# Transposing only the even column tiles of a deformable convolution, and copying the odd ones inside SBUF

## The chip, the cores and the metric

The kernel runs on one core of a Trainium2 chip. A core has a matrix engine (TensorE, PE in the profile), a vector engine (VectorE, DVE), a scalar engine (ScalarE, ACT), a general engine (GpSimd, POOL) and a queue engine (SyncE, SP), and 16 DMA engines that move data between the chip's memory (HBM) and the core's on-chip memory SBUF, or inside SBUF. SBUF has 128 partitions. TensorE writes to a small second memory, PSUM, from which ScalarE or VectorE copies results to SBUF. DMAs are issued from the queues of SP, ScalarE and GpSimd. The metric is the time of one execution on the device in microseconds (us); lower is better.

## The reference

The input `x` is 8 images of 128 channels and 64x64 pixels, in float32. There are two layers, each added to its input. Layer 0 is a group norm, a modulated deformable 3x3 convolution, a batch norm and a ReLU. Layer 1 is a group norm and a routed mixture of 3x3 convolutions. The change touches layer 0 alone. Cut to what matters:

```python
om  = conv3x3(x, off_w) + off_b                 # 27 maps: 18 offsets, 9 masks
py  = off[:, :, 0] + row + ky ; px = off[:, :, 1] + column + kx
val = corner(y0, x0, (1-ly)*(1-lx)) + corner(y0, x0+1, (1-ly)*lx) \
    + corner(y0+1, x0, ly*(1-lx))   + corner(y0+1, x0+1, ly*lx)
val = val * sigmoid(mask)                       # 9 samples for each pixel and channel
y   = einsum('bckhw,ock->bohw', val, w) + b     # then batch norm, ReLU
```

For each pixel and each of nine taps the sample is a bilinear mix of the four pixels around a shifted position, and all 128 channels are mixed alike. The weight of a pixel at distance `d` in one direction is max(0, 1 - |d|).

## The kernel before

**Tiles.** An image is cut into 8 bands of 8 rows (`NB`), each of two halves of `T` = 4 rows. Across, there are `NCOL` = 15 column tiles that begin every 4 columns and are `Q` = 8 columns wide, so that neighbours share 4 columns. A patch of one half and one column tile is 8x8 = 64 pixels, so the two halves of a column tile fill 128 partitions: partition = 64 h + 8 y + x. All samples whose offset stays below 2 pixels (`REACH`) lie inside their patch. A program that finds larger offsets takes another path, which doesn't run here.

**A band.** Five steps lead from the image to the output of a band.

1. `pick` (L748, VectorE, two copies of 128x960) takes the 15 patches of the normalised image in `pads` into one of two `picked` buffers, channels on partitions.
2. `pixels` (L761) turns them with TensorE, one 128x128 transpose for each column tile, in groups of 4, 4, 4 and 3. A group goes into one PSUM bank, `pt` (tag "pc", one buffer, which other work shares), and ScalarE copies it to `xt` (L773). `xt` has pixels on partitions and channels along the row; there are two such buffers.
3. The weights in x come from a table in HBM (`x_table`). `load_x` (L722) reads one row of 9216 bytes for each half and spreads it over 64 partitions, as two GpSimd DMAs, into one of three `x_wts` buffers. `spread` (L738) makes weights of it: ScalarE takes |distance - column of this partition| (the bias `column`), VectorE subtracts 1 and clips at 0. It works on the two halves of the row (`HALVES`) one after the other. The weights in y are loaded by `load_y` (L706), eight GpSimd DMAs a band into one of two `y_wts` buffers.
4. `weights` (L779, VectorE) multiplies both into `s`, for three column tiles at a time, and `sample` (L800) multiplies `xt` by `s` on TensorE: 30 products a band, 60 matmul instructions. ScalarE copies them into `samples` (L820).
5. `conv` (L847) is the convolution proper: nine taps of 128x128 weights (18 matmul instructions for a span of rows), one ScalarE copy to `y`, one SP DMA of `y` to HBM (L869).

**Order.** Everything in this stage is in an order written out by hand. The loop over 64 bands (and one more turn) at L954 samples band `g`, and then runs the convolution of band `g - 1`, with other work placed between its nine steps: the transposes of band `g + 1` at steps 0, 1, 5 and 6 (`PIXELS`), `load_x` of `g + 3` at step 2, the Abs and clip of the halves of band `g + 2` at steps 1, 3, 5 and 7 (`SPREAD`), and `pick` of `g + 2` at step 4. The y loads of `g + 2` are issued during the sampling. The first and last bands of an image have their convolution in two spans. The generator `tables` makes the offset maps and tables of the image after the next, a small piece at every `tick`; it uses all engines, and SP for its DMAs.

**Start.** Before the loop the tables of image 0 are made in one go (L871 to L920), with the first transposes (L694), the first y loads from the SP and ScalarE queues (L697), and the weights of the first band.

Of the kernel before, what the change touches and what calls it, by code (L numbers as in the profile page):

```python
# [47 lines left out]
GT = 3  # L48
NGR = NCOL // GT
M = 3 * T  # L50
WB = W + 2
# [13 lines left out]
def deform_moe_conv(  # L65
# [113 lines left out]
    def dense():  # L179

        with ExitStack() as st:
# [10 lines left out]

            picked = [a1.tile([P, NCOL, 2, Q, Q], F32, name=f"picked{i}") for i in range(2)]
            for t in pads:
# [31 lines left out]

            place_i = a1.tile([P, 2], I32, name="place_i")
            place = a1.tile([P, 2], F32, name="place")
            beside = a1.tile([P, 1], F32, name="beside")
            nc.gpsimd.iota(place_i, pattern=[[REACH, 2]], base=Q - REACH, channel_multiplier=1)  # L230
            for i, n in ((0, T), (1, Q)):
                nc.vector.tensor_single_scalar(
                    place_i[:, i : i + 1], place_i[:, i : i + 1], n - 1, op=ALU.bitwise_and
                )
            nc.vector.tensor_copy(place, place_i)
# [6 lines left out]
            nc.vector.tensor_tensor(place[:, 0:1], place[:, 0:1], beside, ALU.add)  # L242
            nc.vector.tensor_scalar(place[:, 1:2], place[:, 1:2], -1.0, None, ALU.mult)
            in_tile, column = place[W:P, 0:1], place[:, 1:2]

# [60 lines left out]
            def tables(b):  # L306
# [224 lines left out]
                if b == 0:  # L531
                    for g in range(2):
                        pick(g)
                nc.vector.tensor_reduce(
                    most[:, b : b + 1], omr, AX.X, ALU.max, apply_absolute_value=True
# [155 lines left out]
                for i in (3, 0, 4, 1, 2):  # L691
                    masked(i)
                    store_y(i, 1, soon)
                for _ in pixels(0):  # L694
                    pass
                for k in range(2 * T):
                    load_y(0, k, nc.scalar if k in (1, 4, 7) else nc.sync)  # L697
                for _ in statistics(1):
                    pass
                for slots in ((NCOL * T, XROW // XSTEP), (0, 12), (12, 36), (36, NCOL * T)):  # L700
                    spread(0, slots)
                store_x(2, 6, nc.gpsimd)
# [19 lines left out]
            def load_x(g, engine):  # L722

                if g >= len(bands):
                    return
                b, j = bands[g]
                for h in range(2):
                    engine.dma_start(  # L728
                        out=x_wts[g % 3][HALF * h : HALF * h + HALF],
                        in_=bass.AP(  # L730
                            tensor=x_table[b].tensor,
                            offset=x_table[b].offset + (2 * j + h) * XROW,
                            ap=[[0, HALF], [1, XROW]],
                        ),
                    )


            def spread(g, slots=(0, XROW // XSTEP), steps_=(0, 1)):  # L738

                if g >= len(bands):  # L740
                    return
                part = x_wts[g % 3][:, slots[0] * XSTEP : slots[1] * XSTEP]
                if 0 in steps_:
                    nc.scalar.activation(part, part, AF.Abs, bias=column)  # L744
                if 1 in steps_:
                    nc.vector.tensor_scalar(part, part, -1.0, 0.0, ALU.add, ALU.min)  # L746

            def pick(g):  # L748

                b, j = bands[g]  # L750
                for h in range(2):
                    one = pads[b % 2][:, 2 * T * j + T * h : 2 * T * j + T * h + 1, 0:1]
                    nc.vector.tensor_copy(  # L753
                        picked[g % 2][:, :, h],
                        bass.AP(
                            tensor=one.tensor, offset=one.offset,
                            ap=[list(one.ap[0]), [T, NCOL], [W, Q], [1, Q]],
                        ),
                    )

            def pixels(g):  # L761

                xts[g] = a2.tile([P, NCOL, P], F32, name="xt")
                for c0 in range(0, NCOL, 4):
                    n = min(4, NCOL - c0)
                    pt = ps_c.tile([P, 4, P], F32, name="pt", tag="pc")
                    for c in range(n):
                        nc.tensor.transpose(  # L768
                            pt[:, c],
                            picked[g % 2][:, c0 + c].rearrange("p h y x -> p (h y x)"),  # L770
                            ident,
                        )
                    nc.scalar.copy(xts[g][:, c0 : c0 + n], pt[:, 0:n])  # L773
                    yield

            def width(q):
# [23 lines left out]
            def sample(n):  # L800
# [5 lines left out]
                for c in range(GT * q, GT * q + GT):  # L806
                    k = 3 * (T + 2 * (c in (0, NCOL - 1)))
                    for h in range(2):
                        rows = slice(HALF * h, HALF * h + HALF)
                        nc.tensor.matmul(  # L810
                            by_m[:, h, :, at : at + k],
                            lhsT=xts[g][rows, c],
                            rhs=s[rows, :, at : at + k],
                            start=True, stop=True,
                        )
                    at += k
# [102 lines left out]
            for n in range(AHEAD):  # L919
                weights(n, nc.vector if n < AHEAD - 1 else nc.gpsimd)  # L920
            HALVES = (0, 32), (32, 64)
            load_x(1, nc.gpsimd)
# [4 lines left out]
            asked = False  # L927
            PIXELS, BLOCKS, SPREAD = (0, 1, 5, 6), (2, 3, 4, 7, 8), (1, 3, 5, 7)

# [24 lines left out]
            for g in range(len(bands) + 1):  # L954
                b, j = bands[g] if g < len(bands) else (B, 0)
                if j == NB - 2:
                    for _ in made:
                        pass
                    asked, made, means_of = True, iter(()), statistics(b + 2)
                turned = pixels(g + 1) if g + 1 < len(bands) else iter(())  # L960
                if j == NB - 1:
# [13 lines left out]
                for done, _ in enumerate(taps):  # L975
# [5 lines left out]
                    if odd == 0 and part in SPREAD:  # L981
                        half, step = divmod(SPREAD.index(part), 2)
                        spread(g + 2, HALVES[half], (step,))
                    if odd == 0 and j == NB - 2 and part in (0, 1, 2, 4):
# [10 lines left out]
                    if odd == 0 and part == 4:  # L995
                        if g + 2 < len(bands):
                            pick(g + 2)
                        if 3 <= j < 6:
# [3 lines left out]
                for _ in turned:  # L1002
                    pass
                if g == 0:
                    load_x(3, nc.gpsimd)
                    pick(2)
                    for slots in HALVES:
                        spread(1, slots)
                    for n in range(AHEAD):
                        weights(NGR + n)  # L1010
                    for slots in HALVES:
                        spread(2, slots)
                if g == 5:
# [604 lines left out]
```

## Time and profile before

| | |
|---|---|
| Median of 3 runs | 1461.16 us (1460.37 to 1461.41) |
| The profiled execution, its own time | 1462.95 us |
| Its span, first to last instruction | 1461.2 us |
| Mean granted TensorE clock | 0.972 |
| TensorE matmuls, busy | 1339.4 us, 92% of the span |
| VectorE, ScalarE, GpSimd, busy | 996.1, 826.9 and 439.7 us |
| Bytes moved | 227.32 MB, mean 156 GB/s |
| Transposes (L768) | 960 |
| Copies of `xt` (L773) | 256, 142.0 us busy |
| x loads (L728) | 128 of 576 KB, median 7.7 us from issue to landing |
| y loads (L713) | 512 in all queues, 90 KB each |

A line of instructions is read as: source line, engine, operation, tiles written and read, shape, and count; then busy time and mean duration in ns of one; then how long the engine sat idle just before, and what ended that idle time. Matmuls are pipelined, so the durations of neighbours overlap. Idle time of an engine that isn't the bottleneck costs nothing. The rows of digits give the busy share in 40 equal slices of the span, in tenths.

### The profile page before, as it was taken

The page shows a single profiled execution, that of the slowest core. Times are in us where ns is not written, and L with a number is a line of the kernel's source. Part 1 is how long each engine was busy: PE and PEld are TensorE (multiplying, and loading weights), DVE is VectorE, ACT ScalarE, POOL GpSimd, SP SyncE. Part 2 cuts the span into 40 slices and gives each one's busy share as a digit, 9 for nine tenths or more (in the row PEclk, how much of TensorE's full clock was granted, in tenths as well). Part 3 has the DMA queues.
Part 4 walks back from the last instruction along what each step waited for, and adds up shares of the span by engine and source line. Part 5 has one row for each costly group of instructions (what it writes and reads, how often), then busy time and mean ns, then how long its engine had stood idle before and what let it go on. Part 6 is the DMA issues. An engine that isn't in the chain of part 4 may idle for free.

```text
span 1461.2 us, 21972 instructions
## 1 busy us (share of the span) xinstructions
PE 1339.4 (92%) x8002; PEld 766.7 (52%) x8002; DVE 996.1 (68%) x1986; ACT 826.9 (57%) x1117; POOL 439.7 (30%) x745
## 2 busy tenths in 40 slices
PE   4169989999999999999999999999976999999998
PEld 1144556656556656656656566565642444444443
DVE  5546687678668757857866686654528887888872
ACT  2365875777687577668668757866633333232320
POOL 6243333433435234333534433343212101011000
PEclk9579999999999999999999999999997999999999
DMA  4494874884687497577758756677418544565411
GB/s 147 94 187 121 178 182 127 191 209 127 160 212 181 127 204 189 145 175 200 177 131 196 189 147 162 169 186 194 139 39 238 143 125 129 149 173 163 111 44 60
DMA packets 120144, 227.32 MB, mean 156 GB/s; under 512 B 73142, under 2 KB 76370, under 8 KB 111338
## 3 DMA queue, kind: packets, MB, share of 16 engines
q0 software_dynamic: 55024, 137.08, 40.7%
q1 hardware_dynamic: 64795, 88.25, 19.9%
q8 instruction: 65, 1.06, 0.3%
q14 instruction: 53, 0.43, 0.1%
q10 hardware_dynamic: 207, 0.50, 0.1%
HBM read 180.23 MB, written 45.35 MB: 154 GB/s over the span
## 4 chain that ended last, share of the span: by engine, by line
PE 55%; ACT 6%; DMA 5%; issue 5%; DVE 3%; POOL 2%; SPq 0%; DVEq 0%; POOLq 0%; ACTq 0%
PE pc L1530 20%; PE py L859 18%; PE pq L810 10%; PE pt L768 4%; PE pc L453 3%; POOL ywts L713 2%; DMA xwts<-tabx 2%; ACT xwts L744 1%; ACT xt L773 1%; DMA taby<-work 1%; DMA ywts<-taby 1%; ACT pad L340 1%; DMA x<-in_x_dram 1%; ACT om L515 1%; ACT samples L820 1%
## 5 line engine op out<-in xcount | busy, mean ns | idle before, releaser
L859 PE MATMUL py<-samples,dw_sb 128*128 128x512 f32 (+3 forms) x1296 | 573.1, 560 | 7.1 <-ACT y L867 5.3
L713 POOL DMA_DIRECT2D ywts<-taby x504 | 295.9, 608 | 563.5 <-DVE s L794 468.8
L820 ACT COPY samples<-pq 128x864 f32<-128x864 f32 (+1 forms) x320 | 281.3, 976 | 32.0 <-PE pq L810 32.0
L859 PEld LDWEIGHTS py<-samples,dw_sb 128*128 128x128 f32 x1296 | 217.5, 189 | 152.8 <-issue 122.5
L810 PE MATMUL pq<-s,xt 64*128 64x144 f32 (+1 forms) x3840 | 279.7, 299 | 19.0 <-DVE s L794 13.2
L810 PEld LDWEIGHTS pq<-s,xt 64*128 64x128 f32 x3840 | 253.9, 188 | 62.3 <-DVE xwts L746 22.5
L746 DVE TENSOR_SCALAR xwts<-xwts 128x1152 f32<-128x1152 f32 (+2 forms) x130 | 97.4, 749 | 196.8 <-ACT xwts L744 187.3
L794 DVE TENSOR_TENSOR s<-xwts,ywts 128x72 f32<-128x72 f32 (+1 forms) x447 | 199.3, 498 | 43.4 <-PE pq L810 40.1
L773 ACT COPY xt<-pt 128x512 f32<-128x512 f32 (+1 forms) x256 | 142.0, 555 | 143.9 <-PE pt L768 142.7
L768 PEld LDWEIGHTS pt<-ident,picked 128*128 128x128 f32 x960 | 111.2, 141 | 176.3 <-ACT xt L773 110.0
L768 PE MATMUL pt<-ident,picked 128*128 128x128 f32 x960 | 152.5, 279 | 33.7 <-ACT xt L773 31.1
L1530 PE MATMUL pc<-v,u 128*128 128x512 f32 x384 | 174.2, 600 | 6.3 <-DVE v L1437 6.3
L1530 PE MATMUL pc<-v,wmix 128*128 128x512 f32 x384 | 173.1, 596 | 0.0
L744 ACT ACTIVATE xwts<-xwts,place 128x1152 f32<-128x1152 f32 (+2 forms) x130 | 161.0, 1242 | 18.9 <-DMA xwts<-tabx 18.9
L1508 ACT ACTIVATE t<-pc,bmix 128x512 f32<-128x512 f32 x32 | 22.0, 687 | 187.5 <-PE pc L1530 98.9
L1530 PEld LDWEIGHTS pc<-v,u 128*128 128x128 f32 x384 | 71.8, 191 | 92.9 <-issue 83.1
L1530 PEld LDWEIGHTS pc<-v,wmix 128*128 128x128 f32 x384 | 72.0, 189 | 90.9 <-issue 88.9
L867 ACT ACTIVATE y<-py,db_sb 128x512 f32<-128x512 f32 (+3 forms) x72 | 45.8, 636 | 73.3 <-PE py L859 36.4
L728 POOL DMA_DIRECT2D xwts<-tabx x128 | 73.7, 592 | 31.5 <-DMA ywts<-taby 20.2
L753 DVE COPY picked<-pad 128x960 f32<-128x960 f32 x128 | 81.3, 676 | 0.0
L664 DVE TENSOR_TENSOR work<-work,combo 64x576 f32<-64x576 f32 x40 | 29.6, 746 | 44.8 <-ACT work L631 44.8
L945 DVE BATCH_NORM_STATS2 ystats<-y 128x6 f32<-128x512 f32 (+3 forms) x72 | 44.4, 625 | 20.1 <-ACT y L867 20.1
(199 smaller groups left out, 1043.1 us busy)
## 6 DMA issues: line engine op xcount, KB each, us to landing
xwts<-tabx POOLq DMA_DIRECT2D x128, 576.0 KB, 7.7
ywts<-taby POOLq DMA_DIRECT2D x504, 90.0 KB, 3.8
pad<-in_x_dram SPq DMA_DIRECT2D x36, 512.0 KB
out_dram<-yo SPq DMA_DIRECT2D x32, 512.0 KB
yd<-y SPq DMA_DIRECT2D x48, 256.0 KB
pad<-yd SPq DMA_DIRECT2D x16, 512.0 KB
x<-yd SPq DMA_DIRECT2D x16, 512.0 KB
x<-in_x_dram POOLq DMA_DIRECT2D x16, 512.0 KB, 9.1
```

Source lines behind the costliest of these rows:

```text
L713: engine.dma_start(out=y_wts[g % 2][at : at + NR * Q, r].rearrange("p a b c -> p (a b c)"), in_=bass.AP(tensor=y_table[b].tensor, offset=y ...
L728: engine.dma_start(out=x_wts[g % 3][HALF * h : HALF * h + HALF], in_=bass.AP(tensor=x_table[b].tensor, offset=x_table[b].offset + (2 * j + ...
L744: nc.scalar.activation(part, part, AF.Abs, bias=column)
L746: nc.vector.tensor_scalar(part, part, -1.0, 0.0, ALU.add, ALU.min)
L753: nc.vector.tensor_copy(picked[g % 2][:, :, h], bass.AP(tensor=one.tensor, offset=one.offset, ap=[list(one.ap[0]), [T, NCOL], [W, Q], [1, Q]],
L768: nc.tensor.transpose(pt[:, c], picked[g % 2][:, c0 + c].rearrange("p h y x -> p (h y x)"), ident,)
L773: nc.scalar.copy(xts[g][:, c0 : c0 + n], pt[:, 0:n])
L794: engine.tensor_tensor(s[:, :, 3 * at : 3 * (at + k)].rearrange("p m (c x) -> p m c x", x=3), by_x[:, :, c : c + k], by_y[:, :, w : w + k] ...
L810: nc.tensor.matmul(by_m[:, h, :, at : at + k], lhsT=xts[g][rows, c], rhs=s[rows, :, at : at + k], start=True, stop=True,)
L820: nc.scalar.copy(bass.AP(tensor=one.tensor, offset=one.offset + first, ap=[list(one.ap[0]), [M * PLANE, 2], [PLANE, M], [WB + 1, 3], [1, w ...
L859: nc.tensor.matmul(py, lhsT=dw_sb[:, 3 * (2 - yy) + 2 - xx], rhs=samples[g % 2][:, m : m + 3 * n - 2 : 3, xx, 1 : W + 1], start=(i == 0), ...
L1530: nc.tensor.matmul(pc, lhsT=us[j][:, kx], rhs=vs[g][:, rows, kx : kx + W], start=(kx == 0), stop=(kx == 2),)
```

## The change

Neighbouring column tiles share half of their columns: the 8 even tiles together hold every column once, and each odd tile consists of the last 4 columns of one even tile and the first 4 of the next. In the changed kernel `pick` and `pixels` handle the 8 even tiles only. A new function `share` makes the 7 odd tiles from them with eight DMAs, one for each column `x`: for this column it copies 16 partitions (2 halves and 8 rows), 7 tiles of 128 channels each (3584 bytes a partition), to the same partitions of the odd part of `xt`. As the partitions stay the same, an odd tile has its two groups of 4 columns exchanged, and `spread` uses a second bias for odd tiles. Its Abs is split into even and odd tiles rather than into two halves of the row, and the even part into two instructions.

In the loop the transposes are made two bands ahead, at steps 0 and 1 only; `share` is issued on SP's queue at step 3; both parts of the Abs stand at steps 1 and 3, the two clips at 5 and 7; `pick` is made three bands ahead. At the start, the transposes of the first two bands come right after their `pick`, the eight transfers of each are issued from ScalarE's queue, and the first y loads are dealt to SP, GpSimd, ScalarE and GpSimd in turn.

The source of an x load is written as eight groups of eight repeats of the row instead of 64 repeats. The bytes are the same.

```diff
+EVEN = (NCOL + 1) // 2
...
-            place_i = a1.tile([P, 2], I32, name="place_i")
...
+            for i, base, mask in ((0, T - REACH, T - 1), (1, 0, Q - 1), (2, T, Q - 1)):
+                one = place_i[:, i : i + 1]
+                nc.gpsimd.iota(one, pattern=[[0, 1]], base=base, channel_multiplier=1)
+                nc.vector.tensor_single_scalar(one, one, mask, op=ALU.bitwise_and)
...
                     for g in range(2):
                         pick(g)
+                        for _ in pixels(g):
+                            pass
+                    pick(2)
...
-                for _ in pixels(0):
-                    pass
+                for g in range(2):
+                    share(g, nc.scalar)
                 for k in range(2 * T):
-                    load_y(0, k, nc.scalar if k in (1, 4, 7) else nc.sync)
+                    load_y(0, k, (nc.sync, nc.gpsimd, nc.scalar, nc.gpsimd)[k % 4])
...
-                            ap=[[0, HALF], [1, XROW]],
+                            ap=[[0, Q], [0, Q], [1, XROW]],
...
+            def spread(g, tiles=(0, NCOL + 1), sides_=(0, 1), clip=True):
...
+                part = x_wts[g % 3].rearrange("p (c k) -> p c k", c=NCOL + 1)
+                for side in sides_:
+                    first = tiles[0] + (tiles[0] + side) % 2
+                    if first < min(tiles[1], NCOL):
+                        some = part[:, first : min(tiles[1], NCOL) : 2]
+                        nc.scalar.activation(some, some, AF.Abs, bias=columns[side])
+                    if side == 0 and tiles[1] > NCOL:
+                        some = part[:, NCOL]
+                        nc.scalar.activation(some, some, AF.Abs, bias=columns[side])
+                if clip:
+                    some = part[:, tiles[0] : tiles[1]]
+                    nc.vector.tensor_scalar(some, some, -1.0, 0.0, ALU.add, ALU.min)
...
-                            ap=[list(one.ap[0]), [T, NCOL], [W, Q], [1, Q]],
+                            ap=[list(one.ap[0]), [Q, EVEN], [W, Q], [1, Q]],
...
+                for c0 in range(0, EVEN, 4):
...
+            def share(g, engine):
+
+                if g >= len(bands):
+                    return
+                for x0 in range(T):
+                    for side in range(2):
+                        rows = slice(x0 + T * side, P, Q)
+                        engine.dma_start(
+                            out=xts[g][rows, EVEN:].rearrange("p c n -> p (c n)"),
+                            in_=xts[g][rows, 1 - side : EVEN - side].rearrange("p c n -> p (c n)"),
+                        )
...
-                            lhsT=xts[g][rows, c],
+                            lhsT=xts[g][rows, c // 2 + EVEN * (c % 2)],
...
-            PIXELS, BLOCKS, SPREAD = (0, 1, 5, 6), (2, 3, 4, 7, 8), (1, 3, 5, 7)
+            PIXELS, BLOCKS, SPREAD = (0, 1), (2, 3, 4, 7, 8), (1, 3, 5, 7)
...
-                turned = pixels(g + 1) if g + 1 < len(bands) else iter(())
+                turned = pixels(g + 2)
...
-                        half, step = divmod(SPREAD.index(part), 2)
-                        spread(g + 2, HALVES[half], (step,))
+                        step, half = divmod(SPREAD.index(part), 2)
+                        if step:
+                            spread(g + 2, HALVES[half], ())
+                        else:
+                            spread(g + 2, sides_=(half,), clip=False)
+                    if odd == 0 and part == 3:
+                        share(g + 2, nc.sync)
...
-                        if g + 2 < len(bands):
-                            pick(g + 2)
+                        pick(g + 3)
...
                 if g == 0:
+                    share(2, nc.sync)
                     load_x(3, nc.gpsimd)
-                    pick(2)
-                    for slots in HALVES:
-                        spread(1, slots)
+                    pick(3)
+                    spread(1)
```

## The prediction

> **What bounds the kernel now.** I read three views in this order: the slices and costliest groups of the page, busy time by stretch, and the timeline of one band. The page first.
>
> ```profile
> span 1461.2 us, 21972 instructions
> ...
> PE   4169989999999999999999999999976999999998
> ...
> L768 PE MATMUL pt<-ident,picked 128*128 128x128 f32 x960 | 152.5, 279 | 33.7 <-ACT xt L773 31.1 <-DVE picked L753 2.6
> ...
> L744 ACT ACTIVATE xwts<-xwts,place 128x1152 f32<-128x1152 f32 (+2 forms) x130 | 161.0, 1242 | 18.9 <-DMA xwts<-tabx 18.9
> ...
> L753 DVE COPY picked<-pad 128x960 f32<-128x960 f32 x128 | 81.3, 676 | 0.0
> ```
>
> TensorE (PE) is full from slice 4 to the end of the banded stage, near 1066 us; the transposes are 152.5 us of that. PE sat idle before them for 33.7 us only. The view by stretch (length, then busy time and count of PE, weight loads, DVE, ACT, POOL; clock; DMA share; GB/s) takes a heavy band of ScalarE, the two longest kinds, the start, and bands 4 on:
>
> ```profile
> 532.00:547.00 15.00, 14.53 (x96) 8.72 (x97) 9.84 (x24) 13.97 (x21) 5.62 (x10) 1.00 1.01 242
> ...
> 609.70:628.60 18.90, 18.90 (x192) 11.16 (x191) 15.42 (x31) 11.02 (x15) 5.94 (x10) 1.00 0.49 128
> ...
> 72.00:110.00 38.00, 25.95 (x174) 18.26 (x176) 18.50 (x36) 22.99 (x28) 18.92 (x32) 0.77 0.89 182
> ...
> 151.90:1050.00 898.10, 875.14 (x6411) 545.47 (x6410) 614.93 (x1252) 642.93 (x858) 340.16 (x584) 1.00 0.70 173
> ```
>
> PE is busy 875.14 of 898.10 us, so what PE no longer issues is time saved until another engine takes over. Next are ScalarE (0.72 on average, 13.97 of 15.00 in some bands) and the transfers (0.70). At the start, 72 to 110 us, the transfers lead (0.89). One light band on PE:
>
> ```profile
> 774.41 3.67 PE L859 MATMUL py<-samples,dw_sb 128*128 128x512 f32 x8
> 777.92 0.60 PE L768 MATMUL pt<-ident,picked 128*128 128x128 f32 x4
> 778.36 1.04 PE L859 MATMUL py<-samples,dw_sb 128*128 128x512 f32 x2
> 779.24 0.51 PE L768 MATMUL pt<-ident,picked 128*128 128x128 f32 x3
> 779.58 1.92 PE L859 MATMUL py<-samples,dw_sb 128*128 128x512 f32 x4
> ```
>
> From the start of a transpose group to the next convolution matmul: 778.36 - 777.92 = 0.44 us for four, 779.58 - 779.24 = 0.34 us for three. The durations overlap (0.60 for the first), so I price by starts.
>
> **What the Trainium skill says.** "SBUF — State Buffer", Door 1: 64 consecutive partitions reach 8 of 16 ports, measured 196 GB/s. The trace agrees: between 56.9 and 63.0 us, with the first pair of x loads and little else, the view by stretch has 206 GB/s. "DMA: Bandwidth & Descriptors", on why a DMA increments by 16: a transfer uses the largest number of engines up to 16 that divides both slowest dimensions. With 64 groups that is 16 engines a load, with eight groups it is 8. This trace doesn't name engines, so it can't show it; but the first eight y loads, whose source has five groups, move at only 142 GB/s between 63 and 69 us, other traffic included. "Perfetto Trace Analysis", Identifying Dependency Chains: an instruction that waits for several sources may get EventSemaphore instructions ahead of it. The trace has them on PE's queue, 51 ns each.
>
> **The change, part by part.** The sum is made against the profiled span, 1461.2 us (that execution took 1462.95, the median of the runs is 1461.16; span and median may stand for each other here).
>
> *Transposes.* 15 a band become 8. The groups of four and three at steps 5 and 6 of the convolution go, in 62 bands (2 to 63): 62 x (0.44 + 0.34) = -48 us. The groups at steps 0 and 1 stay and serve a band later in the order.
>
> *Stalls at these groups.* A group waits for the ScalarE copy of the group before, in order behind whatever ScalarE has. In the chain of waits at 707.9 to 713.0 us the third copy stands behind four 128x512 normalisations, and PE's last group starts about 1 us late. Over 62 bands the last group costs 0.58 us by starts on average, against 0.34 undisturbed: 62 x 0.24 = 15 us are such stalls. I take -10, bounds 0 and -15, since a faster PE finds ScalarE and VectorE less far ahead.
>
> *ScalarE.* Two copies go (583 + 470 ns). Abs was 2 x 1257 ns; it becomes one strided 128x1152, a 128x144 (414 ns, seen once) and a 128x1008, about 1110 ns scaled: 0.27 us more. Net -0.8 us a band. It still binds in short stretches where it had 13.97 of 15.00 us, some three bands of eight: 22 x 0.2 us, +4. If an Abs is late, the clip on VectorE and then the products `s` are late; both Abs now come earlier (steps 1 and 3, clips 5 and 7).
>
> *VectorE.* `pick` copies half as much, some 0.6 us a band less; nothing on the path, as PE bounds.
>
> *The eight transfers.* 8 x 16 rows x 3584 B = 459 KB a band. Page section 3 gives prices: queue q1 moved 88.25 MB in 19.9% of 1461 us, 303 GB/s; q0 137.08 MB in 40.7%, 230. So 1.5 to 2.0 us of all engines a band; each set of rows, eight partitions apart, reaches half of the ports by the skill's map, so I take 2.0. Issue on SP: 0.32 us is the median of a y store, 0.7 to 0.9 us that of a y load, so 2.6 to 7 us a band; SP mostly waits (518 us for y alone). Behind them stand the y store, the quarter loads and the table stores; the y tile has two buffers, so ScalarE would feel a late store only a convolution later. They are issued at step 3 of band g and read in band g + 2, over 20 us later; landing takes 3.8 us for a 90 KB y load. Priced 0, and if the cover goes, PE waits in each first odd tile.
>
> *Waits on PE.* The first odd tile of each band waits for eight transfers: if two to an instruction, four at 51 ns, 0.2 us; hidden instances show no gap, so 0 to 0.2; I take 0.15: 62 x 0.15 = +9. Behind it stands the whole sampling of the band.
>
> *Transfers' capacity.* 898.10 us hold 59 bands, 15.2 us each at 0.70: 10.7 us. With 2.0 more it is 12.7 of some 14.4. x loads: median 7.7 us to land, a band of slack. Two loads on eight engines each side by side, rather than one after the other on sixteen, lies between no effect and halving the pair; a loss of some us is also open. I put 0 on it in the steady part.
>
> *The start.* Three small iotas and masks instead of one (0.1 to 0.2 us each) lie under the first load of x. Transposes and copies of bands 0 and 1 move ahead into ScalarE's wait (34 to 46 us). ScalarE issues 16 transfers from 51.1 us on: at 0.35 to 0.86 us 5.6 to 13.8 us, against 12.8 us until its first Abs at 63.88. Two y loads and the Abs of band 0 are queued behind; half of the y loads go to POOL's queue, ahead of an x store. Bounds -3 and +3. In band 0 two groups with copies fewer free about 2.7 us on PE and ScalarE, but y(1) holds the products, and band 2's transfers add 2 us to a saturated stretch. Altogether -1, bounds -10 and +7.
>
> Sum: -48 - 10 + 4 + 9 - 1 = -46; 1461.2 - 46 = **1415 us**. Own range 1396 to 1436.
>
> **Rivals.** *More is gained* (0.10): x loads side by side really use all ports, the start loses its 0.89, and waits on PE cost nothing: another -9 - 4 - 10, 1392. For it: the start's idle PE (12 of 38 us); against: the prices of engines sharing a port. *The limit passes to ScalarE* (0.09): if its three busy bands of eight gain nothing and the two long ones, with VectorE at 15.42 of 18.90, only half, then 22 x 0.78 + 15 x 0.39 = 23 us are lost, and 1438 or somewhat more remains. *Nothing changes* (0.03): the gain goes entirely into new waits, 1461. *Slower* (0.12): the transfers become the bound. Place: xt or xwts late before the first products of a band. They bind from 14.4 - 10.7 = 3.7 us a band for the eight transfers, 1.9 times my price, and lose against the kernel before from 15.2 - 10.7 = 4.5 us. At 4.8 us a band is 15.5 against 15.2 us: 62 x 0.3 = +19, 1480. If each of the eight waits for the landing of the last, 8 x 2.8 us (the shortest y landing) = 22 us a band, far above that point. For it: stretches at 1.01 already; against: they pass without PE waiting.
>
> **How the numbers follow.** The likeliest case has 0.66. Its range leaves little out, the larger gain adds some 0.09, the ScalarE case 0.08: 1388 to 1454 holds about 0.8. Faster 0.85, within 0.2% (about what these runs can tell from no change) 0.03, slower 0.12.
>
> **What would show it.** Transposes x512 and copies of xt x128; a light band of 13.2 us instead of 14.0; PE still above 0.95 busy between 150 and 1000 us; no wait of PE for the new transfers; DMA share near 0.85. Wrong if PE waits for xt in every band, if SP's queue holds y stores back so that ScalarE waits, or if the start reaches band 4 more than 8 us off 151.9.

## The result, and the profile after

The changed kernel takes 1574.98 us (median, 1571.47 to 1578.70), the kernel before 1459.49 us in the same session. The ratio is 1.0794 [1.0773, 1.0815]: 115 us slower, where 1415 us was forecast.

The page of the changed kernel. In this kernel the transposes have line 783, the copies of `xt` 788, Abs 751 and 754, the sampling 839, the convolution 888, the eight transfers 800.

```profile
PE   4049797889979897897989789797993999999998
...
L783 PE MATMUL pt<-ident,picked 128*128 128x128 f32 x512 | 80.8, 281 | 5.1 <-ACT xt L788 3.1
...
xwts<-tabx POOLq DMA_DIRECT2D x128, 576.0 KB, 10.5
```

What the change removes is removed: x512 transposes in place of x960, 80.8 us in place of 152.5, and 5.1 us of idle time before them in place of 33.7. But the row of slices, nearly all nines before, now has sevens and eights all through the banded stage, and an x load lands in 10.5 us in place of 7.7. The view by stretch (length, then busy time and count of PE, weight loads, DVE, ACT, POOL; clock; DMA share; GB/s) shows a band that works as forecast, the sixth band of the same image (band 45), and the whole stage:

```profile
845.10:858.20 13.10, 13.10 (x87) 7.87 (x86) 6.45 (x15) 8.79 (x11) 6.46 (x10) 1.00 0.84 168
...
871.40:897.50 26.10, 15.16 (x87) 9.62 (x86) 11.99 (x26) 16.56 (x23) 5.67 (x10) 0.80 0.84 204
...
166.60:1152.90 986.30, 856.83 (x6005) 537.04 (x6004) 580.58 (x1246) 601.36 (x797) 344.12 (x583) 0.93 0.82 185
```

The first is all TensorE, 13.10 us. The second has as many instructions and takes twice as long. An image has eight bands. In the third to seventh image it is the sixth that is stretched, in the fourth to eighth the first; in the second image the fifth takes 24.9 us. The length of a band, from its first sampling matmul to that of the next, averaged over the third to seventh image (first bands over the fourth to eighth):

| kernel | band 0 starts | third to fifth bands | sixth bands | first bands | all 63 bands |
|---|---|---|---|---|---|
| before | 71.7 us | 14.34 us | 14.60 us | 18.31 us | 992.6 us |
| after | 84.1 us | 13.14 us | 26.08 us | 26.06 us | 1083.7 us |

The timeline of TensorE in the stretched sixth band of the changed kernel (start, duration; in brackets the idle time before and what ended it):

```profile
871.42 0.64 PE L839 MATMUL pq<-s,xt 64*128 64x216 f32 x4
883.01 5.63 PE L839 MATMUL pq<-s,xt 64*128 64x144 f32 x56 [10.94 <-DMA xt<-xt]
```

Four matmuls of an even tile, then 10.94 us for a transfer: the odd tile isn't there. Two more lines of the view by stretch take the wait and the time just after it:

```profile
872.00:883.00 11.00, 0.07 (x2) 0.02 (x1) 6.41 (x13) 5.12 (x8) 0.00 (x0) 0.70 1.03 237
883.00:886.70 3.70, 3.69 (x30) 3.70 (x32) 2.29 (x7) 1.92 (x2) 1.28 (x3) 0.50 0.43 142
```

During the wait the DMA engines are full (share 1.03). And the wait is not all that is lost. This band took 13.0 us more than band 43: 10.94 us are the wait, and 2.06 us are the same 87 matmuls being busy for longer (15.16 us in place of 13.10). For 3.7 us after the wait the granted clock was 0.50. Why the odd tile is late stands in SP's own timeline, from two bands earlier:

```profile
845.60 12.61 SPq L565 DMA_DIRECT2D combo<-rowwise  x10
858.25 8.60 SPq L551 DMA_DIRECT2D combo<-colwise  x5
...
868.25 6.96 SPq L800 DMA_DIRECT2D xt<-xt  x8
```

The eight of band 45 go out from 868.25 to 875.21 us, though the band begins at 871.4. Ahead of them stand the fifteen gathers of the offsets for the next image's tables (L565 and L551), which keep SP for 21.2 us. The kernel before had the same gathers, with nothing urgent behind:

```profile
758.02 6.47 SPq L561 DMA_DIRECT2D combo<-rowwise  x10
764.54 9.29 SPq L547 DMA_DIRECT2D combo<-colwise  x5
```

There they took 15.8 us. The waits of SP's own queue tell where the difference comes from (us in total, times, longest). First a line for 838 to 890 us of the changed kernel, then one for its whole span:

```profile
SPq L565 <- DMA xt<-xt: 5.5, 2, 3.5
```

```profile
SPq L800 <- DMA xt<-xt: 36.9, 22, 5.8
```

Two gathers waited for 5.5 us in all until earlier transfers had landed, and over the span transfers waited for transfers. An issue on SP can thus be late because an earlier one hasn't landed. All waits of SP's queue that a landing ended come to 211 us (122 waits) in this kernel and to 21 us (23 waits) in the kernel before.

The view of the engines' waits sums it up; first the changed kernel:

```profile
POOL ywts L717 <- DMA taby<-work: 87.3, 6, 16.2
...
PE pq L839 <- DVE s L823: 57.1, 12, 10.6
ACT xwts L751 <- DMA xwts<-tabx: 54.9, 18, 6.5
...
PE pq L839 <- DMA xt<-xt: 42.5, 4, 11.2
```

and the kernel before:

```profile
POOL ywts L713 <- DMA taby<-work: 62.0, 5, 13.2
...
ACT xwts L744 <- DMA xwts<-tabx: 18.9, 7, 7.2
...
PE pq L810 <- DVE s L794: 13.2, 4, 4.4
```

So the direct wait for the transfers is one part only; table stores, x loads and the weights `s` are later too. The start is a third place. ScalarE's queue in the changed kernel:

```profile
50.63 7.51 ACTq L800 DMA_DIRECT2D xt<-xt  x9
...
69.62 5.67 ACTq L800 DMA_DIRECT2D xt<-xt  x7
...
77.08 0.41 ACT L754 ACTIVATE xwts<-xwts,place 128x144 f32<-128x144 f32 x1 [25.77 <-DMA xt<-xt]
```

Sixteen transfers held ScalarE's queue from 50.6 to 75.3 us, and the first Abs came at 77.08 us. It wasn't the issuing that took so long. The view of line L800 gives the time of one issue on SP and on ScalarE (shortest, median and longest, in ns):

```profile
L800 SPq DMA_DIRECT2D xt<-xt x496: 486/587/2637, 93.1 to 1154.2; - x166
L800 ACTq DMA_DIRECT2D xt<-xt x16: 493/600/1297, 50.6 to 74.7; - x16
```

Between the ninth and the tenth transfer ScalarE's queue stood still for 11.5 us, until a y load that SP had issued at 58.2 us had landed.

### The profile page after: what moved, and what is told of

It reads as the page before. It is cut to its first block, busy times and chain, and to the rows that moved or that the text cites. A ratio compares the mean times of both kernels' runs of the same rounds, so it can differ in the third digit from the quotient of the medians.

```text
span 1569.7 us, 22061 instructions
## 1 busy us (share of the span) xinstructions
PE 1318.1 (84%) x7554; PEld 755.8 (48%) x7554; DVE 960.6 (61%) x1985; ACT 783.8 (50%) x1055; POOL 446.7 (28%) x751
## 3 DMA queue, kind: packets, MB, share of 16 engines
q0 software_dynamic: 63536, 137.48, 42.4%
q1 hardware_dynamic: 80532, 116.45, 26.5%
## 4 chain that ended last, share of the span: by engine, by line
PE 41%; DMA 26%; issue 10%; DVE 7%; SPq 7%; ACT 5%; POOL 2%; DVEq 0%; POOLq 0%; ACTq 0%
PE py L888 14%; PE pq L839 11%; PE pc L1562 9%; DMA xt<-xt 8%; DMA pad<-in_x_dram 6%; SPq L800 4%; PE pc L454 3%; DMA combo<-rowwise 3%; PE pt L783 2%; DMA xwts<-tabx 2%; DMA combo<-colwise 2%; DMA x<-in_x_dram 2%; ACT xwts L751 2%; SPq L565 2%; SPq L551 2%
## 5 line engine op out<-in xcount | busy, mean ns | idle before, releaser
L888 PE MATMUL py<-samples,dw_sb 128*128 128x512 f32 (+3 forms) x1296 | 556.7, 563 | 12.3 <-ACT y L896 10.5
L839 PE MATMUL pq<-s,xt 64*128 64x144 f32 (+1 forms) x3840 | 306.5, 316 | 132.7 <-DVE s L823 57.1
L839 PEld LDWEIGHTS pq<-s,xt 64*128 64x128 f32 x3840 | 277.3, 204 | 177.6 <-issue 74.5
L888 PEld LDWEIGHTS py<-samples,dw_sb 128*128 128x128 f32 x1296 | 229.8, 191 | 215.6 <-issue 180.5
L751 ACT ACTIVATE xwts<-xwts,place 128x1152 f32<-128x1152 f32 (+3 forms) x132 | 152.8, 1161 | 71.2 <-DMA xwts<-tabx 54.9
L788 ACT COPY xt<-pt 128x512 f32<-128x512 f32 x128 | 74.8, 584 | 61.1 <-PE pt L783 58.3
L896 ACT ACTIVATE y<-py,db_sb 128x512 f32<-128x512 f32 (+3 forms) x72 | 45.6, 634 | 118.4 <-PE py L888 72.8
L783 PEld LDWEIGHTS pt<-ident,picked 128*128 128x128 f32 x512 | 60.7, 143 | 75.7 <-ACT xt L788 39.4
L732 POOL DMA_DIRECT2D xwts<-tabx x128 | 79.6, 632 | 57.7 <-DMA ywts<-taby 23.3
L783 PE MATMUL pt<-ident,picked 128*128 128x128 f32 x512 | 80.8, 281 | 5.1 <-ACT xt L788 3.1
L766 DVE COPY picked<-pad 128x512 f32<-128x512 f32 x128 | 48.0, 417 | 1.4 <-PE pt L783 1.4
## 6 DMA issues: line engine op xcount, KB each, us to landing
xwts<-tabx POOLq DMA_DIRECT2D x128, 576.0 KB, 10.5
```

The lines of the kernel that those rows point to most:

```text
L732: engine.dma_start(out=x_wts[g % 3][HALF * h : HALF * h + HALF], in_=bass.AP(tensor=x_table[b].tensor, offset=x_table[b].offset + (2 * j + ...
L751: nc.scalar.activation(some, some, AF.Abs, bias=columns[side])
L783: nc.tensor.transpose(pt[:, c], picked[g % 2][:, c0 + c].rearrange("p h y x -> p (h y x)"), ident,)
L788: nc.scalar.copy(xts[g][:, c0 : c0 + 4], pt)
L839: nc.tensor.matmul(by_m[:, h, :, at : at + k], lhsT=xts[g][rows, c // 2 + EVEN * (c % 2)], rhs=s[rows, :, at : at + k], start=True, stop=True,
L888: nc.tensor.matmul(py, lhsT=dw_sb[:, 3 * (2 - yy) + 2 - xx], rhs=samples[g % 2][:, m : m + 3 * n - 2 : 3, xx, 1 : W + 1], start=(i == 0), ...
```

## The experiments

My theory after this reading: (1) TensorE gains its 50 us as forecast; (2) SP's queue makes the transfers and what stands behind them late; (3) the x loads in eight groups are slower; (4) the start loses 12 us. The main rival: the 29 MB more that the transfers move fill the DMA engines, whatever the order. All ratios are against the kernel before, run alongside.

### One part undone at a time

*The x loads back to 64 repeats.*

```diff
-                            ap=[[0, Q], [0, Q], [1, XROW]],
+                            ap=[[0, HALF], [1, XROW]],
```

> The x loads alone go back to 64 repeats of the row; all else is the changed kernel. If the eight groups slow the x loads (they land after 10.5 us instead of 7.7) and this starves the bands, the time falls below 1500 us and the landing returns to about 8 us. If the queue of SP makes the eight transfers late, or if the added bytes fill the DMA engines, it stays within 15 us of 1575, and x loads still land after 9 to 11 us.

1535.1 us, 1.0518 [1.0494, 1.0543]: 40 us come back, between the two numbers expected. The landing of an x load falls from 10.5 to 8.6 us, the packets of queue q0 (section 3 of the page) from 63536 to 55344 at the same bytes; sixth bands take 22.7 us, first bands 23.8. The loads are a cause, and not the only one.

*The loop's transfers from GpSimd's queue.*

```diff
-                        share(g + 2, nc.sync)
+                        share(g + 2, nc.gpsimd)
```

> The eight transfers of a band are issued from GpSimd's queue in the loop instead of SP's; those of the first two bands stay on ScalarE's. Queue theory (the transfers stand on SP behind fifteen gathers of the tables and come late): the stalls of about 11 us at the sixth band of each image go, 7 x 11 us, and some of the 7 us at the first bands: 1460 to 1500 us. Capacity theory (the 29 MB more fill the engines): the same bytes, so 1555 us or more.

1657.86 us, 1.1338 [1.1318, 1.1359]. The transfers avoid the gathers and meet something worse. Waits of this kernel:

```profile
POOL xt L800 <- DMA xwts<-tabx: 314.9, 73, 9.6
```

Their issue on GpSimd stands still 73 times for the landing of an x load, with later x and y loads queued behind. The bytes are those of the changed kernel; the queue alone makes 83 us. The time fits the capacity theory's range, but for another reason, so this run doesn't decide between the two theories.

*The transfers of bands 0 and 1 from GpSimd, right behind their copies.*

```diff
                     turned_in(nc.sync if b or k == 0 else nc.gpsimd, k, *where)
+                if b == 0:
+                    for g in range(2):
+                        share(g, nc.gpsimd)
...
-                for g in range(2):
-                    share(g, nc.scalar)
```

> The transfers of the first two bands are issued from GpSimd's queue right behind the gathers of the first table, instead of from ScalarE's before its Abs; the loop is the changed kernel's. If ScalarE's 24.7 us of issuing is what moves the first sampling from 71.7 to 84.1 us, the first band begins by 74 us and the time falls by 10 to 13 us, to about 1563. If the x loads are what is late there, it stays above 1570.

1564.79 us, 1.0693 [1.0664, 1.0723], and band 0 starts at 72.8 us: the start was worth 10 us.

*No transfers in the loop.* An odd tile reads its even neighbour (`c // 2` in the sampling's `lhsT`), so the samples of odd tiles are those of other pixels; the transfers in the loop are left out.

> The loop issues no transfers: an odd tile reads its even neighbour, so the samples of odd tiles are those of other pixels. This is the matrix engine's part of the change alone (with the start as changed, 12 us late). If all of the loss comes from the transfers, 1415 + 12 = 1427 us, 1415 to 1440. If the shorter list of transposes or the split Abs loses time itself, above 1450.

1476.3 us, 1.0126 [1.0077, 1.0176]. The transfers cost about 99 us, and yet what is left is slower than the kernel before. Expected was 1427: with the eight-group loads in it, first bands still take 22.4 us, sixth ones 17.6.

### What is left when all three are undone

*No transfers, 64 repeats, start from GpSimd*: the three edits above together.

> The changed kernel without the transfers in the loop (an odd tile reads its even neighbour, so the samples of odd tiles are those of other pixels), with the x rows read in 64 repeats again, and the transfers of the first two bands issued from GpSimd. This is the change's gain on TensorE alone. If the causes add up (gain on TensorE about -55, start 0, x loads 0, transfers 0): 1400 to 1420 us, light bands at 13.1 us, sixth bands at about 14, first bands of an image at 18 to 19. If the groups of the x loads aren't what held the run without transfers at 1476: about 1465, with first bands of an image still at 22 to 26 us.

1436.01 us, 0.9848 [0.9816, 0.9879]. First bands come down to 19.0 us, the third to fifth take 13.15. But the gain is 25 us, not 55: sixth bands take 17.4 us, against 14.6 before.

*The kernel before with x loads in eight groups*, the reverse of the first edit.

> The kernel before with one edit, the source of the x loads read in eight groups of eight. If the grouping by itself slows the loads until their landing is late: 1480 to 1505 us, with bands 8, 16, 24 and so on over 20 us and Abs waiting for xwts<-tabx for some tens of us. If the grouping hurts only in company with the transfers: within 3 us of the kernel before.

1497.42 us, 1.0250 [1.0224, 1.0275]: 36 us from one access pattern, with no transfer near it, though in another place than I expected: first bands are at 18.6 us, the eighth ones of the third to sixth image at 21.4 (15.0 before). The timeline of ScalarE in the eighth band of the fourth image of this kernel:

```profile
605.12 1.25 ACT L744 ACTIVATE xwts<-xwts,place 128x1152 f32<-128x1152 f32 x1 [5.07 <-DMA xwts<-tabx]
606.28 2.92 ACT L340 ACTIVATE pad<-pad,shift,scale 128x512 f32<-128x512 f32 x4
609.11 0.56 ACT L773 COPY xt<-pt 128x512 f32<-128x512 f32 x1
```

and of TensorE there:

```profile
609.72 0.90 PE L768 MATMUL pt<-ident,picked 128*128 128x128 f32 x3 [5.46 <-ACT xt L773]
```

GpSimd issues these loads from 594.5 us on, and Abs starts at 605.1. Behind the waiting Abs, in ScalarE's order, stand four normalisations and the copy of `xt`, for which TensorE waits 5.46 us. A landing that is 2.2 us longer at the median (7.7 to 9.9 us) goes with 5 to 8 us more in each of these four bands.

*All transfers, with the x loads and the start undone.*

> The changed kernel with x rows in 64 repeats and the first two bands' transfers from GpSimd: what is left against the kernel before is the gain on TensorE and the price of eight transfers a band on SP. If the two undone parts add up: 1525 us (1535 less 10), band 0 at 72 to 73 us, sixth bands still at 20 to 24 us. If they overlap: 1530 to 1540.

1519.17 us, 1.0389 [1.0352, 1.0427], band 0 at 71.6 us, near the 1525 us of the two parts added. Against 1436 this is the price of the loop's transfers alone: 83 us. Not all of it is waiting. TensorE is busy for 1317.7 us in this profile and for 1297.1 us in the one without transfers, with the same 7554 matmuls, at mean granted clocks of 0.935 and 0.961; that is 21 us.

### How the transfers cost 83 us

*The gathers spread out.* From the third image on, each gather is followed by three steps of the loop, and the pause after them is shortened.

```diff
                                 in_=by_row[k][outs, 2 * t],
                             )
+                            yield from pause(3 if b > 1 else 0)
...
+                    yield from pause(3 if b > 1 else 0)
-                yield from pause((50, 36)[b] if b < 2 else 44)
+                yield from pause((50, 36)[b] if b < 2 else 1)
```

> As the run before, but from the third image's tables on the fifteen gathers of an image come one at a time, three steps of the loop apart, in place of all at once; the pause after them is shortened by as much. Queue theory (the transfers of the sixth band are late because fifteen gathers stand ahead of them on SP): sixth bands from band 21 on fall from 22 us to 14 to 16, the wait of the matmuls for xt falls from some 75 us to under 30, and the time to 1470 to 1490. Capacity theory (the bytes of these stages fill the 16 DMA engines whatever the order): within 8 us of the run before.

1534.9 us, 1.0511 [1.0484, 1.0538]: 16 us worse than without the edit, outside both ranges, and sixth bands at 25.7 us. The wait for `xt` has gone from that band; waits of this kernel between 570 and 597 us, its sixth band of the fourth image:

```profile
PE pq L842 <- DVE s L826: 8.4, 1, 8.4
DVE combo L615 <- DMA combo<-rowwise: 8.0, 1, 8.0
```

Now the gathers are late: VectorE, in order, waits 8.0 us for one, and its products `s` stand behind. My theory in its narrow form, that the loss is the wait for `xt`, fell here. This edit moves two things, the order on SP and the cover of the gathers, so it doesn't part queue from capacity by itself.

*All transfers issued, none read* (`lhsT` reads `c // 2`, so the odd tiles' samples are of other pixels).

> The run at 1519 us with all its transfers, whose results nobody reads: every odd tile reads its even neighbour, so the samples of odd tiles are of other pixels. If the loss is that TensorE waits for xt: 1440 to 1455, as without transfers. If the transfers harm by what they hold up behind them on SP (gathers, then the tables and the weights made from them): 1490 to 1515, with sixth bands still over 20 us and TensorE waiting for s.

1507.59 us, 1.0319 [1.0290, 1.0347]. No wait for `xt` is left among the waits of TensorE, and still only 12 of the 83 us come back. Sixth bands, which I expected over 20 us, fall to 16.7, but seventh ones go up to 17.5 (13.7 when the transfers are read) and eighth ones to 14.5 (13.1). First bands stay at 24.1 us. GpSimd waits 72.8 us for the table's stores, against 53.2 us without transfers:

```profile
POOL ywts L718 <- DMA taby<-work: 72.8, 7, 14.8
...
PE pq L840 <- DVE s L824: 51.3, 16, 7.3
```

So most of the price is not that the odd tiles come late. By these waits it is what the transfers make late: the gathers, the table's stores behind them on SP, the loads from that table, and the weights. SP's queue itself waits 174 us for landings here, 184 us when the transfers are read and 17 us without them.

*The transfers of two bands in eight left out*, those of the sixth and seventh (which read the even neighbour in place of the odd tile).

> The run at 1519 us (64 repeats, first two bands from GpSimd), but with the transfers of the sixth and seventh band of each image left out; in those two bands an odd tile reads its even neighbour, so their samples are of other pixels. Every other band has its transfers. Queue theory (the loss comes from one place, where the transfers stand in SP's queue with the fifteen gathers of an image, and delays both them and the gathers, and by these the tables of the next image): sixth bands fall from 21 to 26 us to about 17 as without transfers, first bands of an image from 24.5 to 18 to 20, and the time to 1440 to 1460. Capacity theory (the bytes of all bands): no more than the waits for xt itself, 41 us of the sum, spread, so 1500 to 1519.

1474.23 us, 1.0085 [1.0053, 1.0118]. A quarter of the transfers gives back 45 of the 83 us, and sixth bands are at 17.0 us, as without any. That speaks for place and against bytes summed over all bands; the capacity theory had 0 to 19 us. But the queue theory's 1440 to 1460 us was missed too: first bands, which I expected to fall, stay at 24.9 us. How much of what is left is queueing on SP and how much shared DMA engines isn't parted by these runs. The two are tied together: a transfer that lands late on full engines also stops the next issue on SP.

### Why 25 us and not 55, and a faster form

*No transfers: the odd tiles made on VectorE*, with 64 repeats. Each odd tile takes every partition either from the even tile before or from the one after, at the same partition, so two masked instructions do it.

```diff
+                even, odd = xts[g][:, 0:EVEN], xts[g][:, EVEN:]
+                engine.tensor_scalar(odd, even[:, 1:], late_half[:, 0:1], None, ALU.mult)
+                engine.scalar_tensor_tensor(
+                    odd, even[:, 0 : EVEN - 1], late_half[:, 1:2], odd, ALU.mult, ALU.add
+                )
```

> No transfers at all: x rows in 64 repeats, and the odd tiles made by two VectorE instructions a band (the next even tile times a mask of the partitions, then the even tile before times the other mask, plus that), each of 128x896 elements. From 755 ns for the scalar multiply of 128x1152 and about 750 ns for a two-tensor instruction of 576 elements a partition I estimate 0.6 and 1.2 us, 1.8 us a band on VectorE, of which little is on TensorE's path: 1436 plus 5 to 20, so 1440 to 1455 us, under the kernel before. If VectorE then binds in every light band (13.9 us instead of 13.1): 1470 or more.

1467.88 us, 1.0054 [1.0035, 1.0074], a miss between the two cases: VectorE doesn't bind in the third to fifth bands (13.15 us), but sixth bands take 20.5 us. ScalarE there, at the end of the band before:

```profile
538.13 1.26 ACT L754 ACTIVATE xwts<-xwts,place 128x1152 f32<-128x1152 f32 x1 [1.79 <-DMA xwts<-tabx]
...
540.38 0.68 ACT L638 ACTIVATE work<-work 64x576 f32<-64x576 f32 x1
```

and VectorE, waiting for the second of these:

```profile
541.10 0.75 DVE L671 TENSOR_TENSOR work<-work,combo 64x576 f32<-64x576 f32 x1 [6.19 <-ACT work L638]
```

Abs waits for its load. Behind it stand the tents of the next image's table, two instructions (L634, L638) that make max(0, 1 - |d|); the table's product on VectorE waits 6.19 us for the tents; the rest of VectorE's work, `s` at the end of it, stands behind that product.

*The same, with Abs two steps later* and the clips at steps 7 and 8.

```diff
-            PIXELS, BLOCKS, SPREAD = (0, 1), (2, 3, 4, 7, 8), (1, 3, 5, 7)
+            PIXELS, BLOCKS, SPREAD = (0, 1), (2, 3, 4, 7, 8), (3, 5, 7, 8)
```

> The run with the odd tiles made on VectorE (1468 us), with the four steps that finish the x weights put two steps later in a band: Abs at steps 3 and 5 and the clip at 7 and 8, in place of 1, 3, 5 and 7. In that run's sixth band ScalarE's Abs, waiting 1.8 us for an x load, stands ahead of the tents of the next image's table; VectorE waits 6.2 us for the tent with the weights s queued behind, and TensorE 5.4 us for s. If this order of Abs and tents is why the gain of TensorE isn't all realised: sixth bands fall from 20 to 21 us to 15 to 17 and the time to 1440 to 1455. If the tables are late whatever the order (the steps of the loop are shorter, while the loads and stores of the tables take as long as before): 1462 to 1470.

1432.03 us, 0.9793 [0.9769, 0.9817]: 28 us faster than the kernel before and 36 us faster than the same form with Abs early. Page of this kernel:

```profile
PE   4169988999999999999999999999947999999998
...
L801 DVE TENSOR_SCALAR xt<-xt,late_half 128x896 f32<-128x896 f32 x64 | 43.8, 684 | 73.6 <-ACT xt L791 73.6
...
L802 DVE SCALAR_TENSOR_TENSOR xt<-xt,late_half 128x896 f32<-128x896 f32 x64 | 73.7, 1151 | 2.3
```

The nines are back; 1.8 us of VectorE a band do what eight transfers did, beside TensorE's work. Sixth bands take 16.5 us, all 63 bands 955.2 us against 992.6. In ScalarE's timeline of the same place the first tent now stands ahead of Abs:

```profile
530.17 0.78 ACT L634 ACTIVATE work<-combo,steps 64x576 f32<-64x576 f32 x1
...
531.57 1.24 ACT L754 ACTIVATE xwts<-xwts,place 128x1152 f32<-128x1152 f32 x1
```

*The same, with band 1's odd tiles made after band 0's weights.*

```diff
-                for g in range(2):
-                    share(g, nc.vector)
+                share(0, nc.vector)
...
+                share(1, nc.vector)
```

> As the run before, but the odd tiles of the second band are made after the first band's weights in place of before them: two VectorE instructions of 0.67 and 1.15 us off the way to band 0. 1 to 2 us less than the run before if VectorE sets that start; the same if the loads do.

1438.07 us, 0.9854 [0.9813, 0.9895]; band 0 starts at 76.9 us, against 75.6. No gain, so nothing shows that VectorE's two instructions set that start.

*The later Abs on its own* in three other kernels: the changed kernel, the one with the x loads and the start undone, and the kernel before.

> The changed kernel with one edit, the four steps of the x weights at steps 3, 5, 7 and 8 in place of 1, 3, 5 and 7. If the place of the Abs steps (ScalarE held by a late x load, tents behind it) is what the late transfers and loads act through: 1500 to 1530 us. If late transfers and loads act on their own: 1555 to 1575.

> The run at 1519 us (all transfers, x rows in 64 repeats, first two bands' transfers from GpSimd) with the same edit. The gain of the edit without transfers was 36 us (1468 to 1432). If it is the same here: 1480 to 1490, so the transfers still cost some 50 us and this form of the change is slower than the kernel before. If the transfers delay the gathers themselves: 1505 to 1519.

> The kernel before with the same edit alone (its own order of the four steps kept). If the edit helps any form of the kernel: 1435 to 1450. If it only mends what the shorter bands of the change upset: within 5 us of the kernel before.

1565.58 us, 1.0706 [1.0681, 1.0731]; 1512.32 us, 1.0334 [1.0288, 1.0381]; 1459.24 us, 0.9990 [0.9974, 1.0007]. The edit gives 9 and 7 us where the transfers are, and nothing measurable in the kernel before. It mends what the shorter bands upset, or the two instructions added to VectorE (no run parts these), and isn't what the transfers act through. Against 1432 us, transfers in their best form here (1512 us) cost 80 us more than two VectorE instructions.

## Why the prediction was wrong, point by point

**Transposes, -48.** Right, and so is their number and the band of 13.2 us (13.1 to 13.2 measured). The stalls at these groups went as priced or better: the idle time before transposes fell by 28.6 us. What failed was "what PE no longer issues is time saved until another engine takes over": no engine took over in the sense of being full. Without transfers in the loop and with the other two parts undone, VectorE and ScalarE are busy for 65% and 68% of 150 to 1050 us and the DMA share is 0.73, and still about half of the gain was missing (1436 us), in sixth bands above all. That the shorter bands meet waits of fixed length there is my reading; what the runs show is that the order of Abs and tents was worth 36 us in one such form and nothing in the kernel before.

**"Priced 0, and if the cover goes, PE waits in each first odd tile."** This step lost most: 83 us. Its cover was "issued at step 3 of band g and read in band g + 2, over 20 us later", and "SP mostly waits (518 us for y alone)". The 518 us are a sum over the whole run. In the fourth and fifth band of an image the gathers keep SP for 21.2 us, about the whole cover, and 5.5 us of that are waiting for earlier transfers to land, a wait that the sum of issue times didn't have. The prices themselves held: 8 x 0.59 us of issue a band lie within "2.6 to 7 us", and the share of queue q1 rose from 19.9% of 1461.2 us to 26.5% of 1569.7 us, 125 us or some 2.0 us a band. And what I listed behind the transfers (y store, quarter loads, table stores) left out the fifteen gathers. What the transfers hold up is the larger part: unread transfers still cost 71 us.

**Transfers' capacity, and the slower rival.** The rival (0.12) had the right side and the right first sign, xt and xwts late before the first products, but the wrong mechanism. It put the point at 3.7 us a band everywhere; the third to fifth bands run at 13.1 us with all transfers in them, and two bands in eight hold 45 of the 83 us. Shared engines still have a part that isn't measured apart: the DMA share is 1.03 while band 45 waits, and the packets of an x load (9216 B) took 629 ns on average before and 653 with 64 repeats and the transfers left in. The eight groups alone make it 682, both together 709.

**x loads, "I put 0".** +36 us in the kernel before, 40 us in the changed one. The Trainium skill, "DMA: Bandwidth & Descriptors", Rules for kernel authors, says that an outermost dimension below 16, such as a leading zero-stride broadcast, confines the whole transfer to at most that many engines; I used that rule, and then put nothing on two such loads side by side. The run decides: landing 7.7 to 9.9 us. No trace here names the engines. "A band of slack" was wrong too: GpSimd issues a load when its earlier waits end, 10 us before its Abs in the example above.

**The start, -1.** +12.4 us (84.1 against 71.7), outside my bounds of -10 to +7. The term that failed is the 5.6 to 13.8 us for sixteen issues on ScalarE. The price of one issue was right, 0.60 us at the median for 0.35 to 0.86; left out were the waits between the issues for earlier DMAs to land, above all the one of 11.5 us, so that the sixteen took 24.7 us. With these transfers issued from GpSimd, band 0 starts at 72.8 us. Band 4 starts at 166.6 us, beyond the 8 us that I had named as a sign of being wrong.

**ScalarE, +4.** As a sum of busy time right in size: 826.9 us became 783.8, 0.7 us a band. As an order it was wrong, though I wrote that "both Abs now come earlier": I followed the Abs that is late to the clip and the products, and not to the tents that stand behind it on ScalarE. **Waits on PE, +9.** Not there as a small price in every band: the third to fifth bands became 1.20 us shorter, more than the 0.78 of the transposes.

**Sum.** Transfers 83, x loads 40 and the start 10 make 133 of the 139 us between 1575 and 1436; the other 6 are not assigned, as the parts were measured in different company. Of the 46 us that the forecast had as the whole gain, 25 remain.

## What to carry to other kernels

Before a transfer is called hidden, list what is queued ahead of it on its issuing engine in the busiest band, and what is queued behind it with who waits for that, and ask what each issue has itself to wait for; an engine's idle sum tells none of this. A schedule counted in steps gets less cover from each step when the steps get shorter, so after a saving look for instructions that wait at the head of an in-order queue (here Abs ahead of the tents) and move them back. And where source and destination share a partition, a masked instruction on a half-idle engine can replace transfers altogether.

## What the runs showed of the hardware that I had not expected

- A row of issues takes longer than its issues. One transfer of 56 KB over sixteen strided partitions took 0.59 us to issue on SP and 0.60 us on ScalarE (medians), and eight took 4.9 us on SP where nothing held them up (860.49 to 865.41 us of the kernel at 1519 us). Yet the eight of band 45 took 7.0 us, and sixteen in a row on ScalarE 24.7 us, because the queue stood still until earlier DMAs had landed.
- A wait of TensorE cost more than its length. After 10.94 us of waiting in band 45 the granted clock was 0.50 for 3.7 us more, and the band's matmuls were busy for 2.06 us longer. That the wait lowered the clock is not tested.
- Two loads of 576 KB that differ only in how 64 repeats are written, `[0, 64]` or `[0, 8], [0, 8]`, land in 7.7 and 9.9 us, the latter with 8192 more packets at the same bytes.
- GpSimd's issue of a transfer waited 73 times for x loads issued earlier on that queue to land, 314.9 us in all.
